# A two-level Strassen product in matrices one to three of an RGCN layer, beside the index that sorts its edges

## The chip, the cores and the metric

The kernel runs on one core of a Trainium2 chip. The time is that of one execution on the device, in microseconds (us). One execution was also recorded by the hardware profiler. Its lines name the engines: PE is TensorE (matrix products; PEld are its weight loads), DVE is VectorE, ACT is ScalarE, POOL is GpSimd, and SP issues transfers. PSUM is the memory into which PE writes its products, in eight banks of 512 float32 columns.

## The reference

There are 1250 nodes with 1024 features and 20000 edges, each with a source, a destination and one of 8 types. All numbers are float32.

```python
h = relu(layernorm(x))                       # 1250 x 1024
u = h @ root + bias
for r in range(8):                           # one weight per type of edge
    mask = (edge_type == r)
    sums = segment_sum(h[src] * mask, dst)   # 1250 x 1024
    u += (sums / max(count(mask, dst), 1)) @ weight[r]
z = concatenate([u, h], 1) @ w_gate + b_gate
return x + tanh(u) * z + h * (1 - z)
```

## The kernel before, in words

**Products first, edges after.** Since (A·h)·W is A·(h·W), the kernel computes y_r = h·W_r for all nodes and stores it in DRAM, then gathers the rows of y by edge with an indirect DMA, weights them and adds them up per destination. There are 11 matrices of 1024×1024: s = 0 to 7 are the relations, 8 is the root, 9 and 10 are the halves of the gate's weight. The list `fac` holds a `Factors` for each, with its four quarters (B11 to B22) and the sums of them (t1 to t4) that Strassen's method needs, in nine buffers `w0` to `w8`.

**One product.** The nodes lie in ten blocks of 128. A call of `product` takes two blocks (i and i + 5) against one matrix, as a Strassen product of the Winograd form: seven quarter products (A11, A12, S1, S2, S4, S3 and A22, named by their left factor) of 512×512. Each is four matmuls of 128×128 by 128×512, issued by `add` (L404). There are five products a matrix: i = 0 to 3 form two pairs, (0, 1) and (2, 3), and i = 4 is alone ("fifth pair" in the title of the change, "lone" in the code). After each quarter product ACT copies it from PSUM into a row tile (L428, L452, L463, L483, L513) or DVE adds it in.

**The second level.** Two products of a pair have the same right factors, so one quarter product of both, a 2×2 arrangement of blocks, can again be done by Strassen: seven small products, each two matmuls of 128×256 (`Second.add`, L217), in place of eight matmuls of 128×512. Class `Second` does so with A12·B21 for all matrices s ≥ 1. Class `Third` does it with S4·B22, and class `First` with A11·B11, both only for s > `EARLY` = 3 (`thirds(s)`, `next_first`). Each has sums of left and right blocks that DVE makes (`sums`, `next_sums`, `left`, `right`; 256 or 512 columns wide), and small products that are spread over the two products of the pair as "fills": a call of `fill["first"]`, say, follows the quarter product of that name. `First.early` runs at the end of the product before the pair (so in the lone product for the next matrix's first pair, and in i = 1 for the second pair), and `First.late` in the pair's first product. In `late`, ACT copies a small product into both halves of a bank (L353), and the next small products add to it. `Third.first` (called `q.first`) writes a small product into one bank, has ACT copy it out (L295), does another, and adds or overwrites the first bank with a third.

**The order of the work.** Each engine runs its instructions in the order of the program, which is written out by hand: `step(s, i)` calls `product`, and after each quarter product or fill `product` calls `between(j)`, with j counting up within the product. `beside(j)` puts the loads of the next matrix and DVE's sums there (`make_t1` to `make_t4`, 2048 columns wide), and then calls the work that lies beside the products.

**The index.** In matrices 0 to 3 that work is the index, a generator that does one piece per call. For each of 39 groups of 512 edges: `one_hots` (ACT, four instructions at L1023 and one at L1025), `load_keys` (two transfers on SP: `k_bc` and `l_bc`), `as_bf16` (ACT, L1069), end of the call; `look` (PE, L1091, needs `to_lo`), `count` (PE, L1037), `pick` (DVE, L1099), `add_counts` (DVE), `residue`, `place` (DVE, L1107 and L1112, then indirect DMAs on POOL at L1130), `to_los` (ACT, L1083 and L1084), end of the call. So calls of a first kind (here call A) and of a second (call B) alternate. After the groups comes `order`, which sorts the nodes by their number of edges: `places` is twenty DVE instructions (L1175), two per call. Then `rows_and_weights` writes the order to DRAM and reads the slots by it. The function `on` skips the calls (i, j) = (0, 0) and (4, 5).

**PSUM.** Four banks `ps` rotate, two `ps_b` (from `lead()`) hold the sums that run through a product, `ps_n` and `ps_q` are one bank each. While the index runs, `ps_q` is the index's own: the left half free, `look` and `count` in the right half. Later it serves `Third.first`.

Of the kernel before, what the change touches and what calls it, by code (L numbers as in the profile page):

```python
# [19 lines left out]
def tile_rgcn_highway(  # L20
# [109 lines left out]
    class Factors:  # L130
# [13 lines left out]
        def load_first(self, k=slice(0, KQ)):  # L144
            old = self.old
            if old is None:
                free = wbuf
                self.place = dict(b11=free[0], t3=free[1], b22=free[2], t1=free[3], t2=free[4],
                                  b21=free[5], t4=free[6])
                self.spare = free[7:]  # L150
            else:
                p = old.place
                self.place = dict(b11=old.spare[0], t3=old.spare[1], b22=p["b11"], t1=p["t1"],
                                  t2=p["t2"], b21=p["b22"], t4=p["t3"])
                self.spare = [p["b21"], p["t4"]]
            p = self.place
            self.of = {A11: p["b11"], A12: p["b21"], S4: p["b22"], S1: p["t1"], S2: p["t2"],
                       S3: p["t3"], A22: p["t4"]}
            self.load(0, 0, p["b11"], k=k)
# [26 lines left out]
    class Second:  # L186
# [22 lines left out]
        def left(self):  # L209
            nc.vector.tensor_add(self.s1, self.a21, self.a22)  # L210
            nc.vector.tensor_sub(self.s2, self.s1, self.a11)
            nc.vector.tensor_sub(self.s3, self.a11, self.a21)
            nc.vector.tensor_sub(self.s4, self.a12, self.s2)
# [43 lines left out]
    class Third:  # L257
# [31 lines left out]
        def first(self, p):  # L289
            self.b = psum.tile([P, CG, P], F32, name="ps_q", bufs=1).rearrange(  # L290
                "p c k -> p (c k)")[:, :H]
            self.c = bank()[:, :H]
            self.p = p
            Second.add(self, self.b, self.a11, self.b11, True)
            nc.scalar.copy(self.p[:, :H], self.b)  # L295
            Second.add(self, self.c, self.s1, self.t1, True)
            Second.add(self, self.b, self.s2, self.t2)
            nc.scalar.copy(self.p[:, H:], self.b)

        def last(self, c):  # L300
            Second.add(self, self.b, self.s1, self.t1)
            Second.add(self, self.c0[:, H:], self.s2, self.b22)
            Second.add(self, c[:, :H], self.a22, self.t2)
# [5 lines left out]
        def fifth_to(self, to):  # L309
            nc.vector.tensor_add(to[:, H:], to[:, H:], self.c)  # L310

# [76 lines left out]
    def product(aop, w, to, between=lambda j: None, last=None, pieces=1, whole=True,  # L388
                fill=None, second=None, third=None, inner=None, first=None, early=None, own=(),
                aside=None):  # L390
# [34 lines left out]
        def p7():  # L425
            d = c21 if third is None else aside()
            add(b, S3)
            nc.scalar.copy(d, b)  # L428
            nc.vector.tensor_add(c22, c22, d)  # L429
            done()  # L430
            filled("seventh")
            return d
# [7 lines left out]
        def p2():  # L440
            a = held("ps_q")
            add(a, A12, True)
            nc.vector.tensor_add(c11, c11, a)
            done()

        def p1():
            if first is None:
                b = lead()
                add(b, A11, True)
            else:  # L450
                b = first.late() if inner.holds else first.to1
            nc.scalar.copy(c11, b)  # L452
            done()
            filled("first")
            return b

        def p5(c=None):
            if c is None:
                c = inner.hold() if inner and inner.holds else held("ps_n")
                add(c, S1, True)  # L460
            else:
                add(c, S1, ks=range(KQ // 2, KQ))
            nc.scalar.copy(c22, c)  # L463
            done()
            filled("fifth")
            return c

        if first and inner.holds and early is None and "first" not in fill:
            c = inner.hold()
            add(c, S1, True, ks=range(KQ // 2))  # L470
            b = p1()
            p5(c)
        elif first and inner.holds:
            c = p5()
            b = p1()
        else:
            b = p1()
            if second:
                second()
                p2()  # L480
            c = p5()
# [4 lines left out]
        if whole and not third:  # L486
            p3()
            d = p7()
            if not second:
                p2()  # L490
        else:
            def then():
                inner.then(c)
                done()
                filled("third")

            if early:
                then()
            d = p7()
            if third:  # L500
                last(d, 0)
            if not inner:
                p3()
            elif not early and not inner.holds:
                then()
        if early:
            early()
        if pieces == 1:
            add(b, A22)
            if last:  # L510
                last(b, 0)
            else:
                nc.scalar.copy(c21, b)  # L513
        else:
            for j in reversed(range(pieces)):
                at = slice(j * Q // pieces, (j + 1) * Q // pieces)
                b = bank()
                add(b, A22, True, at)
                last(b[:, at], at.start, d[:, at])
        done()  # L520
        filled("fourth")
# [12 lines left out]
    def thirds(s):  # L534

        return s > EARLY

    waiting, waiting_third, waiting_first = {}, {}, {}
    at_call = [0, 0]

    def next_first(s, i):

        if thirds(s) and i == 1:
            return s, 2
        if thirds(s + 1) and i == NP - 1 and s + 1 < NM - 1:
            return s + 1, 0
        return None

    def step(s, i, between=lambda j: None, second=None):
# [23 lines left out]
        def beside(j):  # L573
            at_call[:] = i, j
            new = fac[s + 1]
            if i == 0 and s > 0 and j == int(thirds(s)):
                fac[s].make_t4()
            if two and i == 0:
                sums(j)
            if q and i % 2 == 0 and j == 3:  # L580
                waiting_first[s, i].fifth_to()
                q.sums()
# [5 lines left out]
            if coming and i > 1 and j == 2:  # L588
                first_sums()
            if two and (i, j) == (1, 6):  # L590
                Second(fac[s], 2).left()
            if (s, i, j) == (0, 0, 3) or (s > 0 and (i, j) == (3, int(thirds(s)))):
# [18 lines left out]
        def sums(j):  # L611
# [3 lines left out]
            for k in {2: (0, 1), 4: (2, 3)}.get(j, ()) if s > EARLY else (j,) if j < 4 else ():  # L615
                e.right(k)
            if j == (5 if s > EARLY else 4):
                e.left()
# [13 lines left out]
        if two:  # L632
# [46 lines left out]
            else:  # L679
# [4 lines left out]
                inner=q, first=waiting_first.get((s, i - i % 2)) if two else None,  # L684
                early=early if coming else None, own=("ps_q",) if s > EARLY and not two else ())
# [73 lines left out]
    def rows_and_weights(g):  # L759
# [16 lines left out]
        for d in range(ND):  # L776
            rows_of(idx[:, g, d, :], table_rows, node_key[:, g, d:d + 1])
            if d % 2:
                yield

    with ExitStack() as early:
# [155 lines left out]
        pid = ix1.tile([P, 1], F32, name="pid")  # L937
        less_pid = ix1.tile([P, 1], F32, name="less_pid")
# [4 lines left out]
        q_bank = psum.tile([P, CG, P], F32, name="ps_q", bufs=1).rearrange("p c k -> p (c k)")  # L943

        def columns():
# [54 lines left out]
            nc.vector.tensor_single_scalar(less_pid, pid, -1.0, op=OP.mult)  # L1000
            yield

        def slots(ix):
# [7 lines left out]
            counted = q_bank[:, H:H + CG * NHI].rearrange("p (c b) -> p c b", b=NHI)  # L1011
            looked = q_bank[:, H + CG * NHI:H + 3 * CG * NHI].rearrange(
# [5 lines left out]
            def one_hots(j):  # L1018
# [13 lines left out]
                now[j] = dict(is_lo=is_lo, is_at=is_at)  # L1032
# [18 lines left out]
            def load_keys(j):  # L1051
                c0, m = j * CG, len(chunks(j))
                for name, of in (("k_bc", keys_dram), ("l_bc", los_dram)):
                    t = now[j][name] = ix.tile([P, CG, P], I32, name=name, bufs=3)
# [24 lines left out]
            def to_los(j):  # L1079

                m, o = len(chunks(j)), now[j]
                to_lo = o["to_lo"] = ix.tile([P, CG, P], BF16, name="to_lo")
# [54 lines left out]

            for j in range(ng + 3):
                for f, of in ((one_hots, j), (load_keys, j - 1), (as_bf16, j - 2),
                              (None, None), (look, j - 3), (count, j - 1), (pick, j - 3),  # L1140
                              (add_counts, j - 1), (residue, j - 2), (place, j - 3),
                              (to_los, j - 2), (None, None)):
# [5 lines left out]
        def order():  # L1148

            with tc.tile_pool(name="sort", bufs=1) as sp:  # L1150

                nc.gpsimd.iota(ids, pattern=[[P, ND]], base=0, channel_multiplier=1)
                ids_f = sp.tile([P, ND], F32, name="ids_f")
                nc.vector.tensor_copy(ids_f, ids)
# [12 lines left out]
                for _ in range(4):  # L1167
# [14 lines left out]
                for g in range(G):  # L1182
                    yield from places(g)
                    if g == 0:
                        for _ in rows_and_weights(0):
                            pass
# [66 lines left out]

        def index():
# [11 lines left out]
        while going[0]:  # L1266
            s, i = next(steps)

            def on(j):

                if s > 0 and (i, j) in ((0, 0), (NP - 1, 5)):
# [7 lines left out]
    with ExitStack() as edges_part:  # L1279
# [4 lines left out]
        inner_pool = edges_part.enter_context(tc.tile_pool(name="inner", bufs=1))  # L1284
        room = [inner_pool.tile([P, 2, n], F32, name=f"inner{k}")
                for k, n in enumerate((H, H, P, P))]
        p5_room = inner_pool.tile([P, H], F32, name="inner4")
# [146 lines left out]
        while s <= EARLY:  # L1434
            step(s, i)
            s, i = next(steps)

        def beside_group():

            for _ in range(4):  # L1440
                yield
            passes_over()
            yield
            yield from rows_and_weights(1)
            yield
            yield
# [341 lines left out]
```

## Time and profile before

| what | value |
|---|---|
| runs | 1342.43, 1342.91 and 1347.58 us; median 1342.91 us |
| the profiled execution | 1342.95 us |
| its span | 1341.2 us (1.75 us less than its time) |
| granted TensorE clock | 0.998 of full |
| busy: PE, DVE, ACT, POOL | 1328.3, 931.1, 372.0, 573.8 us |
| matmul records on PE | 4096 (two for each matmul of the kernel in float32) |
| matrix 1 begins, matrix 4 begins | 139.05 us, 510.18 us (its `First.early` 503.30) |
| one matrix from s = 4 on | 115.8 us |
| last `look` of the index; `places` | about 413 us; 440.9 to 476.3 us |

Busy times are sums over the span and say nothing of order. The timeline gives starts and durations in order; where rows of one engine follow without a gap, the distance of the starts is what one row costs it, since a printed duration runs into the next row. The waits of PE name what ended each idle time of PE.

### The profile page before, as it was taken

What the parts mean: (1) busy time and instruction counts of PE and PEld (TensorE: products, weight loads), DVE (VectorE), ACT (ScalarE), POOL (GpSimd) and SP (SyncE); (2) the same over time, 40 slices, a digit from 0 to 9 for tenths busy, and PEclk for the clock granted to TensorE, in tenths of its full rate; (3) what the DMA queues carried; (4) which work ended last, traced back from release to release, by engine and by line L of the source; (5) the groups of instructions that cost most, each with busy time, mean ns of one, the idle gap of its engine ahead of it and who ended that gap; (6) DMA issues with size and microseconds to landing.
All of it is one profiled execution on the core that took longest, in us unless ns stands there. A gap on an engine that the chain in (4) does not pass through costs nothing.

```text
span 1341.2 us, 13172 instructions
## 1 busy us (share of the span) xinstructions
PE 1328.3 (99%) x4096; PEld 709.1 (53%) x4096; DVE 931.1 (69%) x1763; ACT 372.0 (28%) x786; POOL 573.8 (43%) x509
## 2 busy tenths in 40 slices
PE   9999999999999999999999999999999999999997
PEld 5444455455445545655655565565556556554443
DVE  7753744654572855347887978887778799867875
ACT  3334556465641111211121211122121111221210
POOL 0000454555556256201454645436355565725631
PEclk9999999999999999999999999999999999999999
DMA  8744487956872361133739778868778967879961
GB/s 313 275 182 158 85 138 154 215 87 110 168 177 30 101 172 46 51 127 126 246 118 334 236 251 324 313 222 279 274 265 297 344 202 241 287 272 286 345 170 59
DMA packets 104317, 270.92 MB, mean 202 GB/s; under 512 B 20100, under 2 KB 22354, under 8 KB 104112
## 3 DMA queue, kind: packets, MB, share of 16 engines
q1 hardware_dynamic: 44048, 119.85, 30.9%
q0 software_dynamic: 44064, 118.20, 28.1%
q10 hardware_dynamic: 16128, 31.98, 7.4%
q8 instruction: 32, 0.52, 0.2%
q14 instruction: 45, 0.37, 0.1%
HBM read 212.63 MB, written 75.49 MB: 215 GB/s over the span
## 4 chain that ended last, share of the span: by engine, by line
PE 89%; DMA 4%; issue 3%; DVE 2%; POOL 1%; ACT 0%; POOLq 0%; SPq 0%; DVEq 0%; ACTq 0%
PE ps_b L404 45%; PE ps L404 18%; PE ps L217 12%; PE ps_n L404 5%; PE ps_b L217 2%; PE ps_q L217 2%; PE ps_q L404 2%; PE ps_n L217 1%; DMA got<-y,idx 1%; DMA l_bc<-los_dram 1%; PE ps L369 1%; DMA hr_dram<-row 1%; DMA h_op<-in_L_gnn_b_gate_dram 0%; POOL out_dram L720 0%; DVE u L1320 0%
## 5 line engine op out<-in xcount | busy, mean ns | idle before, releaser
L404 PE MATMUL ps_b<-w,h_op 128*128 128x512 f32 x1560 | 701.9, 595 | 1.1 <-ACT row L483 0.8
L404 PEld LDWEIGHTS ps_b<-w,h_op 128*128 128x128 f32 x1560 | 291.6, 190 | 329.3 <-issue 318.0
L1315 POOL DMA_INDIRECT got<-y,idx x193 | 249.9, 1295 | 309.3 <-DVE u L1320 187.6
L1320 DVE SCALAR_TENSOR_TENSOR u<-got,w_of,u 128x1024 f32<-128x1024 f32 (+1 forms) x193 | 246.7, 1281 | 35.8 <-DMA got<-y,idx 33.3
L404 PE MATMUL ps<-w,h_op 128*128 128x512 f32 (+1 forms) x592 | 263.4, 588 | 1.0 <-ACT row L463 1.0
L1130 POOL DMA_INDIRECT table<-row_col,at_i x157 | 165.3, 1053 | 180.8 <-DVE at_i L1126 119.5
L404 PEld LDWEIGHTS ps<-w,h_op 128*128 128x128 f32 x592 | 111.3, 190 | 125.0 <-issue 120.8
L429 DVE TENSOR_TENSOR row<-row 128x512 f32<-128x512 f32 x53 | 36.6, 691 | 81.3 <-ACT row L428 81.2
L428 ACT COPY row<-ps_b 128x512 f32<-128x512 f32 x53 | 31.0, 585 | 199.5 <-PE ps_b L404 199.5
L513 ACT COPY row<-ps_b 128x512 f32<-128x512 f32 x49 | 28.6, 584 | 200.9 <-PE ps_b L404 179.7
L404 PE MATMUL ps_n<-w,h_op 128*128 128x512 f32 x176 | 80.1, 592 | 0.0
L217 PE MATMUL ps<-w,w 128*128 128x256 f32 x288 | 71.5, 381 | 0.2 <-DVE w L210 0.2
L483 ACT COPY row<-ps_b 128x512 f32<-128x512 f32 x54 | 31.6, 585 | 136.8 <-PE ps_b L404 136.6
L217 PE MATMUL ps<-w,h_op 128*128 128x256 f32 x264 | 68.3, 381 | 0.0
L217 PEld LDWEIGHTS ps<-w,w 128*128 128x128 f32 x288 | 54.2, 190 | 21.7 <-issue 14.3
L217 PEld LDWEIGHTS ps<-w,h_op 128*128 128x128 f32 x264 | 49.6, 190 | 24.3 <-issue 18.7
L1112 DVE SCALAR_TENSOR_TENSOR junk<-k_bc,key_col,before 128x128 f32<-128x128 int32 x157 | 54.9, 350 | 4.2
L452 ACT COPY row<-ps_b 128x512 f32<-128x512 f32 x54 | 31.7, 587 | 92.8 <-PE ps_b L404 87.1
L1099 DVE TENSOR_TENSOR own<-ps_q,is_at 128x160 f32<-128x160 f32 (+1 forms) x40 | 12.7, 317 | 62.4 <-PE ps_q L1037 58.1
L404 PEld LDWEIGHTS ps_n<-w,h_op 128*128 128x128 f32 x176 | 33.4, 190 | 39.5 <-issue 38.7
L463 ACT COPY row<-ps 128x512 f32<-128x512 f32 x37 | 21.6, 585 | 106.9 <-PE ps L404 96.8
L1023 ACT ACTIVATE is_lo<-io,less_lo 128x128 bf16<-128x128 f32 x157 | 50.1, 392 | 3.0 <-PE ps L404 2.3
(237 smaller groups left out, 1441.3 us busy)
## 6 DMA issues: line engine op xcount, KB each, us to landing
y<-row SPq DMA_DIRECT2D x72, 512.0 KB
w<-in_L_gnn_weight_dram ACTq DMA_DIRECT2D x21, 1024.0 KB
w<-in_L_gnn_weight_dram SPq DMA_DIRECT2D x10, 1024.0 KB
k_bc<-keys_dram SPq DMA_DIRECT2D x39, 256.0 KB
l_bc<-los_dram SPq DMA_DIRECT2D x39, 256.0 KB
w<-in_L_gnn_w_gate_dram ACTq DMA_DIRECT2D x6, 1024.0 KB
h_dram<-h_op SPq DMA_DIRECT2D x9, 512.0 KB
u<-in_L_gnn_bias_dram SPq DMA_DIRECT2D x9, 512.0 KB
```

The lines of the kernel that those rows point to most:

```text
L217: nc.tensor.matmul(p, a[:, k, :], b[:, k, :], start=(fresh and k == 0), stop=(k == 1), skip_group_check=True)
L404: nc.tensor.matmul(b[:, at], aop[:, i, k, :], w.of[i][:, k, at], start=(fresh and k == 0), stop=(k == KQ - 1), skip_group_check=True)
L428: nc.scalar.copy(d, b)
L429: nc.vector.tensor_add(c22, c22, d)
L452: nc.scalar.copy(c11, b)
L483: nc.scalar.copy(c12, b)
L513: nc.scalar.copy(c21, b)
L1023: nc.scalar.activation(is_lo[:, i, :], io, AF.Abs, bias=less_lo[:, c0 + i:c0 + i + 1])
L1112: nc.vector.scalar_tensor_tensor(junk, o["k_bc"][:, i, :], key_col[:, c:c + 1], before, op0=OP.is_equal, op1=OP.mult, accum_out=rank[:, c: ...
L1130: ins = nc.gpsimd.indirect_dma_start(out=table[:, :], out_offset=bass.IndirectOffsetOnAxis(ap=at_i[:n, c:c + 1], axis=0), in_=row_col[:n, ...
L1315: nc.gpsimd.indirect_dma_start(out=t[:n], out_offset=None, in_=y[g][:, :], in_offset=bass.IndirectOffsetOnAxis(ap=at[:n, d, k:k + 1], axis=0),
L1320: nc.vector.scalar_tensor_tensor(u[:n], t[:n], w, u[:n], op0=OP.mult, op1=OP.add)
```

## The change

- `thirds(s)` and the new `firsts(s)` hold for s > 0: S4·B22 and A11·B11 are done by `Third` and `First` in matrices 1 to 3 as well. The buffers for their sums (`room`, `p5_room`) are allocated from the start.
- `ps_q` is shared in these matrices: `Third.first` uses the left half, the index the right half. Where it is shared (`apart`), the third small product starts anew instead of adding, and DVE adds what ACT's copy gave before.
- At some calls (`SHARED`) the index's call B waits for a later call; a call is also skipped at (1, 5), and the one at (4, 5) becomes (4, 4).
- `load_keys` is issued two groups earlier, with five buffers for `k_bc`; `to_los` one group earlier, with four buffers for `to_lo`.
- The lone product has a new order: A11, S1, S2, half of A12, S3, the other half of A12, `early`, A22, S4. S1's copy on ACT goes, and DVE reads it from PSUM. B21's buffer is another one.
- The node numbers for the sort (`ids`) are made with the first constants; `order` waits seven calls instead of four ahead of `places`, and does `rows_and_weights` for both groups itself.
- DVE's sums of `Second` are made at other calls (`left` in two parts, `right` at 2 and 5, `make_t4` at 1).

```diff
         def first(self, p):
-            self.b = psum.tile([P, CG, P], F32, name="ps_q", bufs=1).rearrange(
-                "p c k -> p (c k)")[:, :H]
+            self.apart = bool(q_bank)
+            self.b = (q_bank[0] if self.apart else psum.tile([P, CG, P], F32, name="ps_q", bufs=1)
+                      .rearrange("p c k -> p (c k)"))[:, :H]
...
             Second.add(self, self.b, self.a11, self.b11, True)
             nc.scalar.copy(self.p[:, :H], self.b)
             Second.add(self, self.c, self.s1, self.t1, True)
-            Second.add(self, self.b, self.s2, self.t2)
-            nc.scalar.copy(self.p[:, H:], self.b)
+            Second.add(self, self.b, self.s2, self.t2, self.apart)
+            if self.apart:
+                nc.vector.tensor_add(self.p[:, H:], self.p[:, :H], self.b)
+            else:
+                nc.scalar.copy(self.p[:, H:], self.b)
...
     def thirds(s):
-        return s > EARLY
+        return s > 0
+
+    def firsts(s):
+        return s > 0
...
-        if thirds(s) and i == 1:
+        if firsts(s) and i == 1:
             return s, 2
-        if thirds(s + 1) and i == NP - 1 and s + 1 < NM - 1:
+        if firsts(s + 1) and i == NP - 1 and s + 1 < NM - 1:
             return s + 1, 0
...
-        if whole and not third:
+        if lone:
+            a = held("ps_q")
+            add(a, A12, True, ks=range(KQ // 2))
+            p7()
+            p2(a)
+        elif whole and not third:
...
+        if lone:
+            add(b, A22)
+            nc.scalar.copy(c21, b)
+            done()
+            p3()
+        elif pieces == 1:
...
-                for name, of in (("k_bc", keys_dram), ("l_bc", los_dram)):
-                    t = now[j][name] = ix.tile([P, CG, P], I32, name=name, bufs=3)
+                for name, of, bufs in (("k_bc", keys_dram, 5), ("l_bc", los_dram, 3)):
+                    t = now.setdefault(j, {})[name] = ix.tile([P, CG, P], I32, name=name,
+                                                              bufs=bufs)
...
+            load_keys(0)
             for j in range(ng + 3):
-                for f, of in ((one_hots, j), (load_keys, j - 1), (as_bf16, j - 2),
+                for f, of in ((one_hots, j), (load_keys, j + 1), (as_bf16, j - 2),
                               (None, None), (look, j - 3), (count, j - 1), (pick, j - 3),
                               (add_counts, j - 1), (residue, j - 2), (place, j - 3),
-                              (to_los, j - 2), (None, None)):
+                              (to_los, j - 1), (None, None)):
+                    if f is look:
+                        while at_matrix[0] and at_call in SHARED:
+                            yield
...
-                for _ in range(4):
+                for _ in range(7):
                     yield
...
                 for g in range(G):
                     yield from places(g)
-                    if g == 0:
-                        for _ in rows_and_weights(0):
-                            pass
+                    for _ in rows_and_weights(g):
+                        pass
...
+        SHARED = ([1, 0], [1, 3], [1, 4], [3, 0], [3, 4], [3, 5])
...
-                if s > 0 and (i, j) in ((0, 0), (NP - 1, 5)):
+                if s > 0 and (i, j) in ((0, 0), (1, 5), (NP - 1, 4)):
                     return
```

## The prediction

> **What bounds the kernel now.** I read the page first: the busy times, then the chain that ended last.
>
> ```profile
> span 1341.2 us, 13172 instructions
> PE 1328.3 (99%) x4096; PEld 709.1 (53%) x4096; DVE 931.1 (69%) x1763; ACT 372.0 (28%) x786; POOL 573.8 (43%) x509
> PE 89%; DMA 4%; issue 3%; DVE 2%; POOL 1%; ACT 0%; POOLq 0%; SPq 0%; DVEq 0%; ACTq 0%
> ```
>
> PE is busy for 99% of the span, and the chain is PE's. Time comes from PE's own work or from new gaps in it. Then PE's waits (us in total, times, longest): few, and all small.
>
> ```profile
> PE ps L696 <- POOL eps L698: 1.4, 1, 1.4
> PE ps L404 <- ACT row L463: 1.0, 1, 1.0
> PE ps L369 <- DVE h_op L833: 0.8, 1, 0.8
> PE ps_b L404 <- ACT row L483: 0.8, 1, 0.8
> PE ps_q L1091 <- ACT to_lo L1084: 0.6, 1, 0.6
> ```
>
> The stages that the change touches are matrices 1 to 3 (139 to 480 us) and the head of matrix 4. By stretches (PE, PEld, DVE, ACT, POOL busy, each with its count):
>
> ```profile
> 135.00:250.00 115.00, 115.00 (x414) 57.39 (x413) 63.87 (x268) 66.62 (x162) 60.92 (x59) 1.00 0.73 135
> 365.00:480.00 115.00, 115.00 (x335) 56.27 (x334) 72.87 (x174) 29.24 (x63) 57.39 (x50) 1.00 0.45 101
> 480.00:595.00 115.00, 115.00 (x352) 65.99 (x351) 50.79 (x100) 21.40 (x43) 42.15 (x37) 1.00 0.29 93
> ```
>
> The last stretch is matrix 4, which has the quarters already: ACT works 21 us of 115 there, but 67 in matrix 1, where the index lives. So the scheme is to be moved to where ACT has three times the work.
>
> **What PE saves.** PE's timeline in matrix 4 (start, us, line, shape, count); starts are the true spacing, since a printed duration overlaps its neighbour.
>
> ```profile
> 504.16 1.03 PE L217 MATMUL ps<-inner,inner 128*128 128x256 f32 x4
> 505.02 1.03 PE L217 MATMUL ps_b<-w,h_op 128*128 128x256 f32 x4
> ...
> 506.75 3.60 PE L404 MATMUL ps_b<-w,h_op 128*128 128x512 f32 x8
> 510.18 1.88 PE L404 MATMUL ps_n<-w,h_op 128*128 128x512 f32 x4
> ```
>
> From 506.75 to 510.18 are 3.43 us for four matmuls of 512 columns (two records each): 0.8585 each. From 504.16 to 505.02 are 0.865 for two of 256: 0.4325. A Strassen over a pair of quarter products replaces 8 wide matmuls by 14 narrow. Three matrices, two pairs, two products (S4 B22, A11 B11) make 12: 96 wide out (82.4 us), 168 narrow in (72.7). PE gains 9.76 us. By the printed durations of the same rows (3.60 for four, 1.03 for two) it would be 86.4 − 86.5, nothing; but these hold each row's run-out over the next row's start, once per row, so the narrow rows are charged twice as often. I take the starts: the rows follow one another without a gap, so their spacing is what PE pays.
>
> The page Perfetto Trace Analysis of the Trainium skill, under Optimizing Tensor Performance, speaks against this: larger matmuls are more efficient, and independent groups should rotate through different PSUM banks. The first half of the rule the spacing does not show (0.4325 is 0.504 of 0.8585); by the second half, each of the six products in the bank shared with the index would wait for the index's readers.
>
> **What else moves.** DVE gets per Strassen four sums of 256 columns (0.34 apart) and four of 512 (0.60): 3.8 us, 45 in all, so about 79 of 115 us in matrix 1. On average there is room. The lone fifth pair loses one ACT copy per matrix (0.58, ACT idle) and splits A12·B21 in halves: no PE work more, nothing gained or lost. Its new `b21` is loaded at the same call as before, now into the buffer that S3 has just read instead of S4's: nothing, since DVE reads it first in `make_t4`, several wide products on. The index loads go two groups ahead on SP, which takes away the 0.6 us wait at L1091 above: −0.6 (there `to_lo` had waited for the load; what PE reads next in that place is the same group's count, which is ready, so nothing new is late). `rows_and_weights(1)` goes forward on POOL, SP and DVE; the index list is complete at 550.0 and the first gather starts at 631.8 after 80.8 idle, so a sort later by 50 us stays covered; without that cover each us late would be a us of gathers late, still beside PE. The shared bank: the first narrow product waits for `add_counts`; pick 0.23 and sum 0.23 after the counts, 0.6 with the hand-over, behind a covering narrow product of 0.865. I take nothing (at the six places at most 0.6 each, 3.6, if DVE is behind).
>
> **What comes late.** ACT runs in its written order. This is its timeline in matrix 1:
>
> ```profile
> 214.30 0.58 ACT L513 COPY row<-ps_b 128x512 f32<-128x512 f32 x1 [3.06 <-PE ps_b L404]
> 214.78 0.72 ACT L1083 ACTIVATE to_lo<-l_bc,less_pid 128x512 bf16<-128x512 int32 x1
> 215.54 0.63 ACT L1084 ACTIVATE to_lo<-to_lo 128x512 bf16<-128x512 bf16 x1
> 216.08 1.26 ACT L1023 ACTIVATE is_lo<-io,less_lo 128x128 bf16<-128x128 f32 x4
> 217.37 0.63 ACT L1025 ACTIVATE is_lo<-is_lo 128x512 bf16<-128x512 bf16 x1
> 217.91 0.24 ACT L1069 CAST s_b<-seen 128x80 bf16<-128x80 f32 x1
> ```
>
> A 512 copy holds ACT for 0.48, `to_los` 1.28 (call B), the one-hots with `as_bf16` 2.09 (call A), a 256 copy 0.26 to 0.37. In the old schedule a copy has 3.4 us or more to its reader on PE. The quarters' chains give it two or three narrow products, 1.7 to 2.6. From the built order, each place where a call stands ahead of such a copy (ACT from the last wide product's end, 0.2 to start, minus PE's own work up to the reader):
> - `q.first` at product 3: copy 0.48, B 1.28, copy 0.26, A 2.09, copy 0.48, copy 0.37: 5.16. PE has index 0.25 and three narrow products, 2.85. Wait 2.3 in matrix 1, 2.2 in matrix 2; in 3 the index is over. 4.5.
> - `q.first` at product 1 (the third narrow product overwrites what the first copy reads): 0.6, 1.75 and 1.65 in matrices 1 to 3. 4.0.
> - `late` at product 2: 0.2, copy 0.48, A 2.09, broadcast copy 0.57 = 3.34, against 1.73: 1.6, 1.5 and 0.25 (a short group). 3.35.
> - `early` ahead of matrix 1, where the skip is not in force (matrix 0): copy 0.2 + 0.48, B 1.28, A 2.09, copy 0.36 = 4.41, against index 0.25 and four narrow products, 3.71: 0.7. At product 1 and ahead of matrices 2 to 4 a call is skipped: 0.
> - Weight loads that could not be fetched ahead at some 8 such waits: about 0.1 each (513.64 has 1.13 where its neighbours have 1.03): 0.8.
>
> The sort's `places` now fall into matrices 3 and 4 (three more yields):
>
> ```profile
> 440.91 1.55 DVE L1175 SCALAR_TENSOR_TENSOR junk<-v_bc,val,one 128x1280 bf16<-128x1280 f32 x1 [6.07 <-DMA v_bc<-val_dram]
> 442.51 1.55 DVE L1175 SCALAR_TENSOR_TENSOR junk<-v_bc,val,one 128x1280 bf16<-128x1280 f32 x1
> ```
>
> Each takes 1.6, two per call, 20 in all, now beside `make_t1` to `make_t4` (2.2 each) around matrix 4's start. Counted along DVE from product 4 of matrix 3, the add to c22 ends near 50 us after that product's start; the copy for A22 behind it on ACT overwrites its operand, and the copies for `Second` and `q.first` stand behind that copy: they end at 51.75, and PE wants the shared product at 49.06. Wait 2.7, and 0.2 more at the sums behind. 2.9; from 0 (DVE ahead by one place) to 6 (two places late).
>
> Sum: −9.8 −0.6 +4.5 +4.0 +3.35 +0.7 +0.8 +2.9 = +5.9. On the profiled execution's 1342.95 (median 1342.91) that is 1348.9; I say 1349.0. If each wait is short or long by a fourth, 15.5 is 12 to 19, and the time 1345 to 1353. While a narrow product waits, PE's whole queue stands behind it, so each such wait is lost in full; ACT and DVE catch up in it, which is why I count each place by itself.
>
> **Rivals.**
> - ACT's backlog stays covered: ACT is idle for 42% of matrix 1, and a PE that waits once finds later copies done. Then only two or three of the places wait, 2 to 4 us, and 1342.95 − 10.4 + 3 = 1335.6 (1333 to 1338). For it: PE waits 5 us in all now. Against it: the copies stand in a fixed order, and 115 us averages hide a tight 5 us stretch.
> - DVE in matrices 1 to 3 becomes the later engine: picks, residues (four of 0.35), table rows and the new sums in one queue. The price is one 2.2 us sum that stands ahead of a sum with a reader within 0.865: it decides once DVE is more than about 1.7 us behind at a pair's start, and with two such places in each matrix, late by that much once more, it costs 2 × 3 × 1.7 = 10 us above the sum: 1359. For it: DVE at 79 of 115. Against it: before, with 73 busy (365 to 480), no PE wait on DVE of size is there.
> - Narrow matmuls do not keep their 0.4325 where PE's loads lie beside other work: the change then doesn't do what it says. The weight load is 190 ns in a record of 216, so 26 ns of margin; if half of the 336 new records lost 26 ns, 4.4 us less gain: 1353.
>
> **How the numbers follow.** Chances: late copies as summed 0.58, covered 0.20, DVE later 0.16, narrow ones dearer 0.06. Half a per cent is 6.7 us, about what a measurement of this kernel can tell from no change: 1336.2 to 1349.6. The first case straddles the upper bound: of its 0.58, 0.33 stay inside and 0.25 pass it. The covered case gives 0.15 faster and 0.05 inside. The others are slower: 0.16 + 0.06. Faster 0.15, same 0.38, slower 0.47. The likeliest case alone is 1345 to 1353; for 8 in 10 I reach into both neighbours, 1335 to 1358: below it lies half of the covered case, above it most of the DVE case, together under 0.2.
>
> **What would show it.** Right: PE's L217 group grows by 336 records, the L404 ones shrink by 192; PE's waits show new lines from ACT's copies at `late` and `q.first`, 1.5 to 2.3 us each, most in matrices 1 and 2, and one at matrix 4's start. Wrong: waits under 1 us each in the sum of 5 (covered), or lines from DVE sums above 10 us in all.

## The result, and the profile after

The changed kernel takes 1359.24 us (median of 4 runs, 1358.92 to 1363.14), the kernel before 1342.67 beside it: 1.013 of it, 95% interval 1.0107 to 1.0154. It is slower by 16.6 us where 6 were forecast, and above the range. A second set gave 1359.33 against 1342.81 (1.0119, 1.0095 to 1.0142).

The page after, span and busy times. PE's busy time is as before although its work is less:

```profile
span 1357.4 us, 13657 instructions
PE 1327.8 (98%) x4240; PEld 739.4 (54%) x4240; DVE 999.2 (74%) x1909; ACT 373.6 (28%) x799; POOL 572.0 (42%) x509
```

The records are right: 4096 − 192 + 336 = 4240. What ended PE's waits (us in total, times, longest; L219 is the narrow matmul that was L217, L414 the wide one that was L404):

```profile
PE ps_q L219 <- ACT row L298: 9.5, 6, 3.3
PE ps_q L219 <- DVE inner L280: 4.1, 1, 4.1
PE ps_b L219 <- ACT ps_b L363: 3.1, 3, 1.5
...
PE ps_q L219 <- DVE seen L1086: 1.0, 2, 0.9
...
PE ps_b L219 <- ACT ps_b L353: 0.6, 1, 0.6
```

These five lines, 18.3 us, are new; the old wait for `to_lo` (0.6) is gone, as forecast. L298 is `q.first`'s copy, L363 the copy in `late`, L353 the one in `early`. In time, three of the waits stand out, since the row behind them lasts 2.08 where its like lasts 1.13:

```profile
344.81 2.08 PE L219 MATMUL ps_q<-inner,inner 128*128 128x256 f32 x4 [2.07 <-ACT row L298]
540.00 2.08 PE L219 MATMUL ps_q<-inner,inner 128*128 128x256 f32 x4 [3.33 <-ACT row L298]
608.01 2.08 PE L219 MATMUL ps_q<-inner,inner 128*128 128x256 f32 x4 [4.08 <-DVE inner L280]
```

By stretches of 1 us around the second of them (PE, PEld, DVE, ACT, POOL busy; the third number from the right is the granted clock):

```profile
538.00:539.00 1.00, 0.00 (x0) 0.00 (x0) 1.00 (x1) 0.95 (x2) 0.69 (x2) 1.00 0.02 1
539.00:540.00 1.00, 0.00 (x0) 0.00 (x1) 0.96 (x3) 0.95 (x4) 1.00 (x1) 0.68 0.56 225
540.00:541.00 1.00, 1.00 (x2) 0.84 (x3) 1.00 (x3) 0.00 (x0) 0.70 (x2) 0.50 0.76 299
...
546.00:547.00 1.00, 1.00 (x3) 0.42 (x2) 1.00 (x1) 0.00 (x0) 0.00 (x0) 0.90 0.00 0
```

While PE still stands the clock drops to half, at 539.4, and it is full again at 546.2: 6.8 us at half, 6.2 of them behind the start of the row, so 3.1 us lost behind a wait of 3.3. Around 344.81 and 608.01 it is at half for 3.4 us each, which costs 1.7 and 1.5. Together 6.3 us that no line of waits shows.

**The account.** The first step common to both, the first half of S1 of matrix 4 into `ps_n`, begins at 510.18 before and at 514.73 after. Up to there: −9.76 for the matmuls, −0.56 for the old wait, −0.25 because the first wide row begins at 8.37 instead of 8.62, +10.94 for the eleven new waits, +1.9 because a wait's printed length begins only when the modelled run-out of the row before ends (0.17 each: 216.24 + 0.865 is 217.10, the row begins at 219.43, and 2.16 is printed), +1.1 for the weight loads behind them (that row lasts 0.97 and not 0.865), +1.7 for the clock: 515.2. From there to the end it is 831.0 before and 842.7 after, 11.7 more: waits of 3.33 and 4.08, their run-outs 0.34, weight loads 0.2, the clock 4.6, less 1.14 for two small old waits (near 1073 and 1110) that are gone, 11.4. So each part of the account closes within half a us, the forecast of the matmuls' gain with it, and the tail from matrix 4 on holds most of what was missed.

### The profile page after: what moved, and what is told of

Read it like the earlier page. It is cut to its first block, busy times and chain, and to the rows that moved or that the text cites. A ratio compares the mean times of both kernels' runs of the same rounds, so it can differ in the third digit from the quotient of the medians.

```text
span 1357.4 us, 13657 instructions
## 1 busy us (share of the span) xinstructions
PE 1327.8 (98%) x4240; PEld 739.4 (54%) x4240; DVE 999.2 (74%) x1909; ACT 373.6 (28%) x799; POOL 572.0 (42%) x509
## 4 chain that ended last, share of the span: by engine, by line
PE 77%; issue 6%; DVE 5%; POOL 3%; ACT 3%; DMA 1%; POOLq 0%; DVEq 0%; ACTq 0%
PE ps_b L414 37%; PE ps L219 13%; PE ps L414 12%; PE ps_n L414 5%; PE ps_q L219 3%; PE ps_b L219 3%; PE ps_n L219 2%; PE ps_q L414 2%; DVE junk L1217 1%; ACT is_lo L1064 1%; DMA h_op<-z_dram,node 1%; POOL node_dram L796 1%; POOL idx L748 1%; POOL out_dram L754 1%; POOL got L748 0%
## 5 line engine op out<-in xcount | busy, mean ns | idle before, releaser
L414 PE MATMUL ps_b<-w,h_op 128*128 128x512 f32 x1464 | 659.4, 595 | 1.0 <-ACT row L497 0.8
L414 PEld LDWEIGHTS ps_b<-w,h_op 128*128 128x128 f32 x1464 | 274.1, 190 | 305.3 <-issue 295.1
L414 PE MATMUL ps<-w,h_op 128*128 128x512 f32 (+1 forms) x448 | 201.1, 591 | 0.1
L414 PEld LDWEIGHTS ps<-w,h_op 128*128 128x128 f32 x448 | 85.3, 192 | 93.7 <-issue 90.4
L414 PE MATMUL ps_n<-w,h_op 128*128 128x512 f32 x224 | 102.6, 594 | 0.0
L219 PE MATMUL ps<-w,h_op 128*128 128x256 f32 x288 | 75.3, 384 | 0.0
L219 PE MATMUL ps<-inner,inner 128*128 128x256 f32 x288 | 73.9, 379 | 0.0
L219 PE MATMUL ps<-w,w 128*128 128x256 f32 x288 | 71.5, 381 | 0.0
L219 PEld LDWEIGHTS ps<-w,h_op 128*128 128x128 f32 x288 | 54.6, 192 | 24.8 <-issue 18.5
L414 PEld LDWEIGHTS ps_n<-w,h_op 128*128 128x128 f32 x224 | 42.2, 190 | 47.3 <-issue 46.6
L537 ACT COPY row<-ps_b 128x512 f32<-128x512 f32 x40 | 23.4, 585 | 157.4 <-PE ps_b L414 128.5
L219 PEld LDWEIGHTS ps<-w,w 128*128 128x128 f32 x288 | 54.2, 190 | 19.9 <-issue 14.4
L219 PEld LDWEIGHTS ps<-inner,inner 128*128 128x128 f32 x288 | 54.7, 190 | 15.1 <-issue 7.9
L439 DVE TENSOR_TENSOR row<-row 128x512 f32<-128x512 f32 x44 | 30.4, 690 | 44.1 <-ACT row L438 44.1
L219 PE MATMUL ps_q<-inner,inner 128*128 128x256 f32 x144 | 40.5, 407 | 13.6 <-ACT row L298 9.5
```

The source lines that it names most:

```text
L219: nc.tensor.matmul(p, a[:, k, :], b[:, k, :], start=(fresh and k == 0), stop=(k == 1), skip_group_check=True)
L414: nc.tensor.matmul(b[:, at], aop[:, i, k, :], w.of[i][:, k, at], start=(fresh and k == 0), stop=(k == KQ - 1), skip_group_check=True)
L439: nc.vector.tensor_add(c22, c if lone else c22, d)
```

## The experiments

The runs were on several chips. On some the kernel before itself takes 1372 to 1380 us. In the traces of the changed kernels there, ACT and DVE pause for up to 15 us at a time in matrices 1 to 3, and the profile names no engine or transfer of the program as the cause ("remote"); the kernel before has no trace from such a chip. So times are only compared with the kernel before on the same chip, and where there are pauses mainly single waits are read.

**1. Four edits, one at a time** (kernel before on that chip: 1372.01 us).

```diff
-            for _ in range(5):            # beside_group, ahead of the counts: e1
+            for _ in range(10):
-                for _ in range(7):        # order, ahead of places: e2
+                for _ in range(4):
```

> The counts of the groups (DVE, beside matrix 4) start five calls later; nothing else changes. Theory: in the changed kernel DVE stands for 17.9 us on the scratch rows and slot numbers that the later sort delays, and PE's 4.08 us wait at 608 us follows from it, with 0.17 of run-out and 1.7 of a halved clock after it: 5.9 us less, about 1353.3 us, and the 4.1 line of PE's waits gone. Rival (PE waits there for DVE's own backlog of sums, not for the index): within 1 us of 1359.2, with the wait still there.

1391.63 us, 1.0132 (1.0105 to 1.0159). The wait for L280 near 608 is not in the trace; the time is covered by the pauses.

> The sort waits four calls instead of seven, as before the change; nothing else is undone. Theory: slot numbers are ready some 10 us earlier, so the 4.1 us wait at 608 goes (5.9 with its clock), and the twenty places leave the head of matrix 4 in part, so the 3.33 us wait at 540 (6.9 with run-out and 3.4 of clock) shrinks or goes: 1346 to 1353 us. Rival (the places only move their delay into matrix 3, where DVE has the new sums too): a wait of 3 us or more appears in matrix 3, and the time is 1356 or more.

1395.14 us, 1.015 (1.0119 to 1.0182). DVE's long wait for the slot numbers is gone too, and with it PE's wait for L280 at its place; the wait at `q.first` of matrix 4 stays (3.45 us). That fits a counts' wait that comes from the later sort, and three calls do not clear the head of matrix 4. The rival's sign, a wait of 3 us or more in matrix 3, is there too (3.56 us for a copy of ACT's at 455.75), but ACT and DVE pause there, so it says nothing.

```diff
...
-                for i in range(m):
-                    nc.scalar.activation(is_lo[:, i, :], io, AF.Abs, ...)
-                nc.scalar.activation(is_lo[:, :m, :], is_lo[:, :m, :], AF.Relu, ...)
+                nc.vector.tensor_tensor(is_lo[:, :m, :], less_lo[...], less_io[...], op=OP.is_equal)
```

> The index's one-hots (five ACT instructions for 512 edges, 1.85 us) are made by one DVE comparison of 512 columns (about 0.6 us) instead. Theory (the copies of the quarters stand behind the one-hots on ACT): the waits for ACT in matrices 1 to 3 go, 0.55 at early, 3.14 at late, 6.2 at q.first, with about 1.4 of run-out and 1.7 of clock: 13 us less, about 1346. Rival (DVE, already at 77 of 115 us there, becomes the late engine with 23 us more): waits for DVE's sums or counts take their place, 1357 or more.

1381.59 us, 1.0066 (1.0041 to 1.0091). In matrices 1 to 3 the waits for the copies in `late` and `early` are gone, and instead the first small product of `q.first` waits for the index's readers of the shared bank: 3.0 (`pick`), 1.4 and 2.05 (`add_counts`). Both theories have a part: the one-hots were the cause, and DVE takes their place.

```diff
-            Second.add(self, self.c, self.s1, self.t1, True)
+            for _ in range(1 + {(2, 3): 2, (4, 1): 3}.get((at_matrix[0], at_call[0]), 0)):
+                Second.add(self, self.c, self.s1, self.t1, True)
```

> PE repeats the second small product of q.first (it starts its bank anew, so the sum is the same) twice in matrix 2 product 3 and three times in matrix 4 product 1: 1.73 and 2.6 us of PE work in idle times of 2.07 and 3.33 us. Theory (the halved clock follows from the idle time itself): the clock stays at 1.00 behind both, 5.1 us less, about 1354.1 us, though PE does more. Rival (the clock drops for another reason, the index or the place): no change, 1359.2 within 1 us, and the clock still at 0.50 behind both.

1394.32 us, 1.0176 (1.0136 to 1.0215): nothing to be read from the time. So two of the four were run again beside the changed kernel.

**2. On a chip without the pauses** (kernel before: 1342.81 us).

> The changed kernel itself once more, as the measure for the three runs beside it. Both theories: 1.013 of the kernel before, 16 to 17 us more than it.

1359.33 us, the measure for the next three.

> The edit of e1_counts_later (the counts beside matrix 4 begin five calls later), beside the changed kernel on the same chip. Theory (PE's 4.1 us wait at 608 comes from DVE standing on the late slot numbers): 5.9 us less than the changed kernel beside it. Rival (DVE's own backlog): within 1 us of it.

1352.12 us, 1.0063 (1.0041 to 1.0086): 7.2 us less than the changed kernel. In changed_again the wait for L280 is 4.93 us, and the half clock behind it costs 2.0; with the run-out that is 7.1. The line is gone from PE's waits, the others are unchanged. The theory holds, and DVE's timeline in the changed kernel shows the mechanism:

```profile
585.31 0.42 DVE L247 TENSOR_TENSOR row<-row,ps 128x256 f32<-128x256 f32 x1
603.61 0.07 DVE L783 MEMSET got<- 128x10 f32 x1 [17.88 <-DMA idx<-table,node_key]
...
607.26 0.69 DVE L280 TENSOR_TENSOR inner<-w 128x512 f32<-128x512 f32 x1
```

DVE does nothing for 17.9 us. The counts' first instruction stands in DVE's order ahead of the quarters' sums (L280), and waits for the slot numbers and for a scratch row that POOL clears behind its gathers of them. In the kernel before DVE comes to the same instruction without a wait:

```profile
574.50 0.07 DVE L749 MEMSET got<- 128x10 f32 x1
```

The slot numbers are complete at 550.0 there, 24.5 us ahead of it. The change makes them some 54 us later (603.9), and DVE comes to the counts only 11 us later (585.7).

> The edit of e4_fill_two_waits (PE repeats a small product in two of its idle times, the sums stay the same), beside the changed kernel. Theory (the halved clock follows from idle time): 5.1 us less than the changed kernel beside it, clock 1.00 behind both places. Rival (another cause): within 1 us of it.

1358.60 us, 1.0117 (1.0097 to 1.0137): only 0.7 less, so by the time the rival holds. The trace says otherwise. The clock at the filled place, and the row that comes 70 us later:

```profile
539.00:540.00 1.00, 1.00 (x5) 0.69 (x4) 1.00 (x3) 0.00 (x0) 0.82 (x1) 1.00 0.38 140
```

```profile
605.70 2.08 PE L219 MATMUL ps_q<-inner,inner 128*128 128x256 f32 x4 [5.79 <-DVE inner L280]
```

The clock stays at 1.00 behind both filled places, and PE is some 3 us earlier behind the second (538.60 against 541.57). 1.3 of them are not the filling's: they come from an unfilled wait near 219, which halved the clock in changed_again and not here. The next wait is longer, 5.79 us instead of 4.93, and more of its half clock lies behind it (3.0 us lost instead of 2.0). In the two profiled executions 2.2 us are left (1358.48 against 1360.72), by the medians 0.7. So the half clock does follow from the idle time, and the next wait and its clock took back 1.9 us of the gain.

Whether a wait of some 2 us halves the clock depends on when it falls. The same wait in the changed kernel and in changed_again, and the clock behind it:

```profile
219.43 1.13 PE L219 MATMUL ps_q<-inner,inner 128*128 128x256 f32 x4 [2.16 <-ACT row L298]
221.00:222.00 1.00, 1.00 (x4) 0.59 (x4) 0.97 (x4) 0.00 (x0) 0.00 (x0) 1.00 0.51 205
219.30 1.13 PE L219 MATMUL ps_q<-inner,inner 128*128 128x256 f32 x4 [2.15 <-ACT row L298]
221.00:222.00 1.00, 1.00 (x4) 0.81 (x3) 0.75 (x3) 0.00 (x0) 0.00 (x0) 0.50 0.76 301
```

Within one trace the drops lie whole steps of 3.413 us apart: 344.81, 539.37 and 607.64 in the changed kernel (57 and 20 steps), 220.53, 346.82, 541.38 and 606.24 in changed_again (37, 57 and 19). Counted back by such steps, the five waits of 2.06 to 2.17 us that halved the clock in the runs without pauses each lie whole within one step; the four that did not are cut by the end of a step, into 1.25 and 0.91, 1.74 and 0.42, 1.17 and 0.99, 1.99 and 0.08. This is read from the traces; no run moved a wait against the steps on purpose.

```diff
+        TIGHT = ([1, 0], [2, 0], [2, 6], [3, 0])
+                    if f is one_hots:
+                        while (at_call in TIGHT if at_matrix[0] else at_call == [4, 4]):
+                            yield
```

> The one-hots' call is put off by a call at the places where it stood ahead of a quarter's copy: (1, 0), (2, 0), (2, 6) and (3, 0) in matrices 1 to 3, and (4, 4) in matrix 0. ACT's work is the same; the index ends some five calls, 15 us, later. Theory (the copies of late and q.first wait behind the one-hots): in matrices 1 to 3 PE's waits for ACT (9.9 us with early) fall below 2, and the clock stays at 1.00 there, so matrix 4 begins 9 to 12 us earlier than in the changed kernel; in matrix 4 the later sort gives some of it back, so 1347 to 1356 against 1359. Rival (the waits come from what ACT does on average, 57 of 115 us, wherever the calls stand): the same sum of waits for ACT at other lines, and matrix 4 begins within 3 us of the changed kernel's.

1370.76 us, 1.0194 (1.0164 to 1.0224), 11 us more than the changed kernel, outside both expectations; but S1 of matrix 4 begins at 507.10 instead of 516.30, 9.2 earlier, as the theory said. PE's waits:

```profile
PE ps L219 <- DVE inner L274: 27.0, 2, 22.3
PE ps_q L219 <- DVE seen L1086: 2.9, 6, 0.9
PE ps_q L219 <- ACT row L298: 2.8, 2, 1.4
```

The waits for ACT fall from 9.9 us to 2.8 in the stages of the index. The later index makes the counts' wait 22.3 us (DVE stands for 27.9), and another of 4.7 us comes at the head of matrix 4. Up to S1 the account closes here as well: 510.18 − 9.76 − 0.56 − 0.31 (an earlier start) + 5.6 of waits + 1.4 of run-outs + 0.8 of weight loads = 507.4.

**3. Three kernels to keep the gain** (on a chip with pauses, kernel before 1373.14 us). The first two hold the one-hots in matrices 1 and 2 only, with the sort after four calls and the counts five calls later; the second keeps the second group's `places` from four calls of matrix 4 besides.

```diff
+        TIGHT = ([2, 0], [2, 6], [3, 0], [1, 0])
+                    if f is one_hots:
+                        while at_matrix[0] in (1, 2) and at_call in TIGHT:
+                            yield
-                for _ in range(7):        # order, ahead of places
+                for _ in range(4):
-            for _ in range(5):            # beside_group, ahead of the counts
+            for _ in range(10):
...
+        AWAY = ([0, 4], [0, 5], [0, 6], [1, 0])        # places_apart alone
+                        while at_matrix[0] == EARLY + 1 and g and at_call in AWAY:
+                            yield
-                for _ in range(3):        # order, behind the last places; places_apart alone
-                    yield
```

> Three edits of the changed kernel together: the one-hots' call put off at (1, 0), (2, 0), (2, 6) and (3, 0) in matrices 1 and 2 only; the sort after four calls instead of seven, so that it ends two calls later than in the changed kernel and not five; the counts five calls later. Theory: matrices 1 to 3 as in hold_onehots, 9 to 10 us less than the changed kernel, the 4.9 us wait for the counts gone, the wait of 3.3 us at the head of matrix 4 (places ahead of the copies' sums) still there with 0.2 of run-out and 1.7 to 3.4 of halved clock: 1344 to 1348 us, no more than 5 above the kernel before. Rival (a later sort always costs PE what the holds gain): 1352 or more.

1398.42 us, 1.0187 (1.0131 to 1.0242). The wait at the head of matrix 4 is 2.93 us; DVE still stands 13.2 us for the slot numbers, and PE 5.0 behind it. Neither expectation can be read from the time.

> As three_holds, and the second group's places are not done at the calls (0, 4), (0, 5), (0, 6) and (1, 0) of matrix 4 but after them. Theory (those calls put DVE behind, and ACT's copies behind DVE): the 3.3 us wait at the head of matrix 4 goes with its clock, and since POOL is busy with the first group's rows meanwhile the slot numbers come no later: 1338 to 1342 us, at or under the kernel before. Rival (DVE is behind through the quarters' own sums and make_t1 to make_t4, not the places): the 3.3 us wait stays, and the time is three_holds' within 1 us.

1401.62 us, 1.0207 (1.0141 to 1.0273). The wait at the head is the same 2.93. But the index is later here, and DVE does all ten of the first group's places, at 542.5 to 569, ahead of the sum that the copies wait for. In the changed kernel the same ten slots hold six of the first group's and four of the second's. So this run doesn't tell places from the quarters' sums. And PE waits 13.2 us for the counts.

The third has the edits of e3_onehots_on_dve and e1_counts_later together.

> The one-hots of the index by one DVE comparison instead of five ACT instructions (as e3_onehots_on_dve) and the counts five calls later (as e1_counts_later). Theory: PE's waits for ACT at late and early go, and DVE, with 23 us more, is late for the bank that it shares with the index (pick and add_counts ahead of the first small product of q.first): 7 to 9 us of waits for DVE in matrices 1 to 3, with the 3.3 us wait at the head of matrix 4: 1347 to 1352 us. Rival (DVE has room for it): no wait of 1 us or more for DVE in matrices 1 to 3, and 1343 or less.

1378.13 us, 1.0044 (1.0011 to 1.0077). Waits for DVE as in e3_onehots_on_dve (3.0, 1.4, 2.1), and the 3.3 at matrix 4.

**4. What the wait at the head of matrix 4 is, and half the change** (kernel before: 1343.01 us). In the changed kernel DVE's places (L1217) stand ahead of the add to c22 (L439), and ACT's copy (L537), with the copies of `Second` and `q.first` behind it, waits for that add:

```profile
535.79 1.55 DVE L1217 SCALAR_TENSOR_TENSOR junk<-v_bc,val,one 128x1280 bf16<-128x1280 f32 x1
537.27 0.69 DVE L439 TENSOR_TENSOR row<-row 128x512 f32<-128x512 f32 x1
538.04 0.59 ACT L537 COPY row<-ps_b 128x512 f32<-128x512 f32 x1 [8.58 <-DVE row L439]
```

```diff
+                        while at_matrix[0] == EARLY + 1 and (at_call[0] == 0 or at_call == [1, 0]):
+                            yield                     # ahead of each of the places
```

> The changed kernel with the counts five calls later and no places at all in matrix 4 from (0, 0) to (1, 0); they go on at (1, 1) and end six calls later. Read at one place, q.first of matrix 4's product 1. Theory (the places at (0, 1) to (0, 3), beside make_t4 and the quarters' sums, put DVE behind): the 3.3 us wait there is gone or under 0.5. Rival (the quarters' sums alone do it): 2.5 us or more. The time as a whole says nothing: the counts then stand for the slot numbers and PE waits for them near 640 us, 5 to 20 us.

1372.51 us in one run, with a wait of 22.7 us for the counts. At the place in question:

```profile
533.99 1.03 PE L219 MATMUL ps<-inner,inner 128*128 128x256 f32 x4
534.85 1.03 PE L219 MATMUL ps_q<-inner,inner 128*128 128x256 f32 x4
```

The rows follow without a gap: the wait is gone. Six places are held back ahead of that add, the last two of the first group and the first four of the second, and it comes at 527.84 instead of 537.27. The later counts alone do not remove the wait (3.33 us in counts_later_again), so the six places were it.

```diff
     def thirds(s):
-        return s > 0
+        return s > EARLY
-        SHARED = ([1, 0], [1, 3], [1, 4], [3, 0], [3, 4], [3, 5])
+        SHARED = ()
+                    if f is one_hots:
+                        while (at_call == [2, 0] if at_matrix[0] else at_call == [4, 4]):
+                            yield
-                for _ in range(7):        # order, ahead of places
+                for _ in range(4):
-            for _ in range(5):            # beside_group, ahead of the counts
+            for _ in range(10):
```

> Only A11·B11 is done by quarters in matrices 1 to 3; S4·B22 there is whole as before, so ps_q is the index's alone and no call B is put off (SHARED empty). The one-hots' call is put off at (2, 0), and at (4, 4) in matrix 0; the sort begins after four calls and lies wholly in matrix 3, the counts as in counts_later_again. Theory: PE saves half, 48 wide against 84 narrow matmuls, 4.9 us, and the old 0.6 us wait; no wait of 1 us or more and no halved clock in matrices 1 to 4; 1337 to 1340 us on a chip where the kernel before takes 1342.8, a ratio of 0.996 to 0.998. Rival (the quarters' copies are late wherever the index runs): waits of 3 us or more in all in matrices 1 to 3, ratio 1.000 or more.

1345.05 us, 1.0011 (1.0000 to 1.0022): the same as the kernel before. S1 of matrix 4 begins at 504.59, 5.6 us earlier than before (4.88 + 0.56 were worked out, and it starts 0.18 earlier), with no wait in matrices 1 to 3. One wait takes it back, the counts once more: DVE comes to them at 542.2 here, 32 us earlier than in the kernel before, and the slot numbers come at 555:

```profile
PE ps L219 <- DVE inner L280: 6.4, 1, 6.4
```

The clock is at half from 557.2 to 564.0, 3.5 us of it behind the wait: 1.75 us lost, with the run-out 8.3 in all.

```diff
-            for _ in range(10):           # a11_alone
+            for _ in range(18):
```

> a11_alone with the counts eight calls later still (18 instead of 10). Theory: of a11_alone's 6.4 us wait at 560 (DVE standing on slot numbers that were ready at 556) and the halved clock behind it nothing is left, and matrices 1 to 4 keep their 5.6 us: 1343.0 - 5.6 - 0.5 (the changes of order without a wait) = 1336 to 1338 us, a ratio of 0.995 to 0.997. Rival (PE waits somewhere else instead, the counts or weights falling on a fuller DVE before the first gathers): a wait of 3 us or more in matrices 4 to 5, ratio 0.999 or more.

> The kernel of a11_counts_late on another chip: there the kernel before took 1372 us and PE waited at many places for nothing that the profile names, so the question is not answered. Theory: ratio 0.995 to 0.997 of the kernel before where that takes about 1343 us, without a wait of 1 us or more in matrices 1 to 4. Rival: a wait of 3 us or more in matrices 4 to 5, ratio 0.999 or more.

> The kernel of a11_counts_late a third time. In its first two traces matrix 4 to the end takes 830.1 us (before: 831.0; a11_alone: 838.3), but the chips paused ahead of that. Theory: where the kernel before takes about 1343, the head of a11_alone (504.6) and this tail make 1336.5, a ratio of 0.995. Rival: 0.999 or more.

All three fell on chips with pauses: 1393.92, 1399.09 and 1394.59 us, 1.0144 (1.0118 to 1.0169), 1.0144 (1.0109 to 1.0178) and 1.0159 (1.0134 to 1.0184) of the kernel before there. In all three traces the wait is gone, no wait of 1 us or more follows in matrices 4 and 5, and from S1 of matrix 4 to the end it is 830.1 to 830.2 us (before 831.0, a11_alone 838.3). With a11_alone's head of 504.6 that makes an estimate of 1336.5 on a chip without pauses; no run showed it, and on the chips with pauses the kernel before is the faster one. Why the pauses cost the changed schedules more was not found.

## Why the prediction was wrong

- **PE's gain** (9.76 us, by the distance of starts): right, within 0.5 us in the changed kernel, 0.3 in hold_onehots, and by the same working the half in a11_alone. The printed durations would have given nothing.
- **Copies behind the index on ACT**: right in kind and place. `late` 1.51, 1.41, 0.22 (forecast 1.6, 1.5, 0.25), `q.first` of product 3 2.16 and 2.07 (2.3, 2.2), `early` 0.55 (0.7). `q.first` of product 1 was over-sized: 0.51, 1.13, 0.34, or 2.0 us against 4.0. With 0.17 of run-out for each, which a printed wait leaves out, all nine are 11.4 us against 12.55.
- **The shared bank**: taken at nothing; it cost 1.0 us in two places, within the bound of 3.6, though one of them took 0.87 and not at most 0.6.
- **The sort at the head of matrix 4**: right. 3.33 us against 2.9, by the chain that was forecast, and the places are its cause (places_after_the_head).
- **The later slot numbers**: this step failed. The prediction looked for their first reader among the gathers, and found 80.8 us of cover. `counts` on DVE reads them long before, with 24.5 us of cover against 54 us of delay, and its place in DVE's order did not move with the sort. That is 4.1 us of wait in the profiled execution, 5.8 with run-out and clock; counts_later_again measured 7.2 for it.
- **The clock**: this failed too, a term missing from the sum, 6.3 us. The prediction priced each wait at its length; in the profile of before no wait of PE is longer than 1.4 us, and none of them shows it. Around a wait of 2 to 6.4 us the clock is at half for 3.4 or 6.8 us, one or two steps of 3.413, which agrees with the window of 3.4 us that the Trainium skill's page TensorE: Matmul & The Clock Gate gives under Part 1. Its rule under "Why this matters for your kernels", no idle gap over some 3 us, is not strict enough here: in the runs without pauses five of nine waits of 2.06 to 2.17 us halved the clock, the same wait near 219 us in one execution and not in another, and none of 1.51 or less did.
- **The rival that named DVE** had the right size (1359) by another way: the price came not from DVE's sums in matrices 1 to 3 but from one wait of DVE's in matrix 4. The measured time is the sum of the first case and of two things in none of the cases: of the 10.2 us between 1349.0 and 1359.2, the clock (6.3) and the wait for the counts with its run-out (4.3) are all, and the other misses cancel to within half a us.

## What to carry to other kernels

When a step is moved later, look for every reader of what it makes on every engine's queue, and above all for one whose place in the order stays where it was; the first consumer one thinks of need not be the first in a queue. Price a wait of PE of 2 us or more with up to another 1.4 to 3.1 us for the clock (what it cost here where it halved), or fill it with repeated work; but a gain ahead of a wait whose end is set elsewhere is kept only in part. Take the cost of pipelined matmuls from the distance of their starts.

## What the runs showed of the hardware

A wait of 2.06 us on PE was enough to halve its clock for 3.4 us where it lay whole within one of the steps of 3.413 us, and one of 2.16 was not where it was cut by a step's end. And the same program takes 2 to 3% longer on some chips: 1372 to 1380 us instead of 1343, and in the changed kernels' traces there ACT and DVE stand for up to 15 us at a time in the stages of the index for something that the profile puts down to no engine and no transfer of the program; what it is stays open.
